# Setting up a graph kernel on one core: constants from few columns on three engines, and the first element's masks, positions and table made during its sort

## The chip, the cores and the metric

The kernel runs on one core of one Trainium2 chip. The metric is the device time of the whole program in microseconds (us). Engines are TensorE (PE, with PEld for its weight loads), VectorE (DVE), ScalarE (ACT), GpSimd (POOL) and SyncE (SP), which issues nearly all DMAs from one queue, in order.

## The reference, cut to what matters

Four layers run over 16 batch elements of 1024 nodes with 64 features and one adjacency matrix per element; each normalises x, applies relu, and adds its result to x. The change is in the first layer, which for every node aggregates weighted quantiles of its neighbours' features:

```python
adj_d = _dilate_adj(adj, mask)           # drops every skip-th neighbour of large rows
valid = adj_d > 0
sv = jnp.sort(jnp.where(valid[..., None], x[:, None, :, :], big), axis=2)
for tau, wt in zip([.25, .5, .75], [.25, .5, .25]):
    pos = jnp.clip(tau * (valid.sum(-1) - 1.0), 0.0)
    lo, hi = jnp.floor(pos), jnp.ceil(pos)
    agg += wt * (gather(lo) * (1 - (pos - lo)) + gather(hi) * (pos - lo))
y = relu((x + agg) @ W1 + b1) @ W2 + b2
```

Layer 1 is a mean over the adjacency, layer 2 an attention of eight heads biased by it, layer 3 a product with it.

## The kernel before, in words

**Order of work.** The program builds its constants, then two generators are woven by shares written by hand: `picks()` makes the first layer for all elements, `layers()` the other three. A scheduler orders the instructions of each engine by data and by buffers; each pool is a ring of buffers under one tag (`b2` has 6, `q4` 2, `a4` 4), so a new tile waits for what used its buffer.

**Constants (L127 to L352).** Selection matrices, identities, shifts and small columns. Nearly all are made by DVE: a pattern from POOL is widened to 128x128, its bits are reversed in integer steps (`bits_reversed`), compared and multiplied; `at_row` builds a column of per-row values by one comparison and one addition a row, then widens it. They use a scratch pool `scr`, which is closed before the main pool `sb` opens on the same memory. Weights are loaded by SP meanwhile; `rev`, the bit-reversed node numbers, is stored to DRAM as `rev_d`.

**First layer of an element.** The features of two elements share the 128 partitions. `ranked` normalises both, transposes them to `sv` and calls `ranks`. This is a bitonic sort of 1024 values per partition on DVE, 55 steps of compare, min and max (L577 to L579). Each step's comparison `sm` is stored to DRAM (`md`). The sorted values are stored as `vs_d`. Then the sort runs backward over the node numbers (`rev`, L609 to L612), reading the comparisons again (`sb`, two buffers of four steps each), which leaves each node's rank. TensorE transposes it; ACT copies it to `rs`, which is stored as `rk_d`. Beside the sort, in shares of two to one, `dilate` makes the thinned adjacency (`left_d`, `rem_d` in DRAM). For the first element both run alone.

Only then come the `stages` of the element: load its rank `rk`; for each half of the nodes, eight pairs of loads `lr` (L517, L521), TensorE's `pn`, and ACT's `valid` (fp8); counts `pm` by a product with ones, evicted as `m` (L640); positions `n`, `kq`, the rows `krow` (twelve ACT copies), `coef`; and from the sorted values `vs` the table `tab` by way of `put`, `u`, `pd` and `df`. `pair_weights` turns rank into weights `cw` (through `e`). `group` then counts with them (`px`, `high`, `low`, `cum`, `c`). The first comparison `le` (L819) with its products `wa` and `wb` opens the steady loop. For later elements stages and sort are spread behind the loop of the element before.

**The lines that the steps touch.** For the first element, before:

```python
els[0] = arrive(0)
for r in background(0):          # sort and dilate
    yield 0.0
for _ in els[0].stages:          # masks, positions, table
    pass
for pp in range(4):
    prepare(els[0], 0, pp)       # cw
for _ in make(els[0], 0, 0):     # first group
    yield 0.05
```

Of the kernel before, what the change touches and what calls it, by code (L numbers as in the profile page):

```python
# [8 lines left out]
F32 = mybir.dt.float32  # L9
# [29 lines left out]
def tile_preln_adj_stack(  # L39
# [87 lines left out]
    scr_i = sc("scr_i", (P, 5, P), I32)  # L127
    scr_f = sc("scr_f", (P, 3, P))
    identf = const.tile([P, P], F32, name="identf")
    make_identity(nc, identf)  # L130
    ident = const.tile([P, P], HP, name="ident")
    nc.vector.tensor_copy(ident, identf)

    rev_i = sc("rev_i", (P, C), I32)
    nc.gpsimd.iota(rev_i, pattern=[[1, C]], base=0, channel_multiplier=C)
    rev_a = sc("rev_a", (P, C), I32)
    rev_b = sc("rev_b", (P, C), I32)
    nc.vector.memset(rev_a, 0)
    for b_ in range(N.bit_length() - 1):
        up = N.bit_length() - 2 - 2 * b_  # L140
        nc.vector.tensor_scalar(
            rev_b, rev_i, 1 << b_, abs(up), op0=OP.bitwise_and,
            op1=OP.logical_shift_left if up >= 0 else OP.logical_shift_right,
        )
        nc.vector.tensor_tensor(rev_a, rev_a, rev_b, OP.bitwise_or)
    rev = sc("rev", (P, C), HP)
    nc.vector.tensor_copy(rev, rev_a)
    rev_d = dram.tile([P, C], HP, name="rev_d")
    nc.sync.dma_start(rev_d, rev)
    minus_i = const.tile([P, P], BF, name="minus_i")  # L150
    nc.vector.tensor_scalar(minus_i, identf, -1.0, None, op0=OP.mult)
# [3 lines left out]
    fmp_i = scr_i[:, 0, :]  # L155
    nc.gpsimd.iota(fmp_i, pattern=[[1, P]], base=0, channel_multiplier=-1)
    fmp = scr_f[:, 0, :]
    nc.vector.tensor_copy(fmp, fmp_i)


    step2 = sc("step2")
    nc.vector.scalar_tensor_tensor(step2, fmp, 2.0, identf, op0=OP.is_equal, op1=OP.subtract)
    dif = const.tile([P, 2, P], HP, name="dif")
    nc.vector.tensor_scalar(dif[:, 0, :], step2, -SPAN, None, op0=OP.mult)
    nc.vector.tensor_scalar(dif[:, 1, :], step2, -1.0, None, op0=OP.mult)
    less = const.tile([P, 2, P], HP, name="less")
    nc.vector.tensor_scalar(less[:, 0, :], identf, -2.0, None, op0=OP.mult)
    nc.vector.tensor_scalar(less[:, 1, :], identf, -FINE, None, op0=OP.mult)

    prow_i = scr_i[:, 1, :]  # L170
    nc.gpsimd.iota(prow_i, pattern=[[0, P]], base=0, channel_multiplier=1)
    fcol_i = scr_i[:, 2, :]
    nc.gpsimd.iota(fcol_i, pattern=[[1, P]], base=0, channel_multiplier=0)
    par_i = scr_i[:, 3, :]


    sel_w = const.tile([P, 2, 2 * BKW], HP, name="sel_w")
    nc.vector.tensor_scalar(par_i, prow_i, 1, None, op0=OP.bitwise_and)
    par = const.tile([P, 2], F32, name="par")
    nc.vector.tensor_copy(par[:, 1:2], par_i[:, 0:1])  # L180
    nc.vector.tensor_scalar(par[:, 0:1], par[:, 1:2], -1.0, 1.0, op0=OP.mult, op1=OP.add)
    par_up = const.tile([P, 2], F32, name="par_up")
    nc.vector.tensor_scalar(par_up, par, UP, None, op0=OP.mult)
    for c2 in range(2):
        cols = slice(c2 * BKW, (c2 + 1) * BKW)
        for i, w in enumerate((2.0, 2.0 * FINE)):
            nc.vector.tensor_scalar(
                sel_w[:, i, cols], fcol_i[:, :BKW], 0.0, w, op0=OP.mult, op1=OP.add
            )
            nc.vector.tensor_scalar(sel_w[:, i, cols], sel_w[:, i, cols], par[:, c2 : c2 + 1], None, op0=OP.mult)  # L190

    def bits_reversed(x, bits, n, name):
        r, u = sc(name + "_r", (P, n), I32), sc(name + "_u", (P, n), I32)
        nc.vector.memset(r, 0)
        for i in range(bits):
            up = bits - 1 - 2 * i
            nc.vector.tensor_scalar(
                u, x, 1 << i, abs(up), op0=OP.bitwise_and,
                op1=OP.logical_shift_left if up >= 0 else OP.logical_shift_right,
            )  # L200
            nc.vector.tensor_tensor(r, r, u, OP.bitwise_or)
        return r


    pblk = scr_i[:, 3, :]
    same = scr_f[:, 1, :]
    fblk = scr_i[:, 4, :]
    nc.vector.tensor_scalar(fblk, fcol_i, 4, None, op0=OP.logical_shift_right)
    fpl = sc("fpl", (P, P), I32)
    nc.vector.tensor_scalar(fpl, fcol_i, 15, None, op0=OP.bitwise_and)  # L210
    fplr = bits_reversed(fpl, 4, P, "fpl")
    ppl = sc("ppl", (P, P), I32)
    nc.vector.tensor_scalar(ppl, prow_i, 15, None, op0=OP.bitwise_and)
    pplr = bits_reversed(ppl, 4, P, "ppl")
    nc.vector.tensor_scalar(pblk, prow_i, 4, None, op0=OP.logical_shift_right)
    nc.vector.tensor_tensor(same, pblk, fblk, OP.is_equal)

    to30 = const.tile([P, 2], I32, name="to30")
    field = sc("field", (P, P))
    nc.vector.tensor_scalar(field, pplr, 15.0, None, op0=OP.is_equal)  # L220
    keep = sc("keep", (P, P))
    nc.vector.tensor_scalar(keep, field, -1.0, 1.0, op0=OP.mult, op1=OP.add)
    nc.vector.tensor_scalar(to30[:, 0:1], pplr[:, 0:1], 15.0, keep[:, 0:1], op0=OP.add, op1=OP.mult)
    nc.vector.tensor_scalar(
        to30[:, 1:2], field[:, 0:1], -65536.0 - 1073741824.0, 1073741824.0, op0=OP.mult, op1=OP.add
# [3 lines left out]
    tri = scr_f[:, 2, :]  # L229
    nc.vector.tensor_tensor(tri, pplr, fplr, OP.is_le)  # L230
    nc.vector.tensor_tensor(tri, tri, same, OP.mult)
    nc.vector.tensor_scalar(tri, tri, 0.5, None, op0=OP.mult)
    nc.vector.scalar_tensor_tensor(tri, identf, -40.5, tri, op0=OP.mult, op1=OP.add)
    nc.vector.tensor_tensor(tri, tri, keep, OP.mult)
    nc.vector.tensor_tensor(field, field, same, OP.mult)
    nc.vector.scalar_tensor_tensor(tri, field, 1.0 / KHI, tri, op0=OP.mult, op1=OP.add)
    nc.vector.tensor_scalar(field, fplr, 15.0, -0.5, op0=OP.is_equal, op1=OP.mult)
    nc.vector.tensor_scalar(field, field, 1.0, None, op0=OP.add)
    nth = const.tile([P, P], BF, name="nth")
    nc.vector.tensor_tensor(nth, tri, field, OP.mult)  # L240
# [3 lines left out]
    nc.vector.memset(sel_t, 0.0)  # L244
    for i in range(2):
        nc.vector.tensor_tensor(sel_t[:, i, 8 * i : 8 * i + 8], pblk[:, 0:8], fcol_i[:, 0:8], OP.is_equal)

    sel_c = const.tile([P, 8], F32, name="sel_c")
    nc.vector.tensor_scalar(pblk, prow_i, 7, None, op0=OP.bitwise_and)
    nc.vector.tensor_tensor(sel_c, pblk[:, 0:8], fcol_i[:, 0:8], OP.is_equal)  # L250
# [3 lines left out]
    fbk = sc("fbk", (P, P), I32)  # L254
    nc.vector.tensor_scalar(fbk, fcol_i, 1, None, op0=OP.logical_shift_right)
    pbk = sc("pbk", (P, P), I32)
    nc.vector.tensor_scalar(pbk, prow_i, 63, None, op0=OP.bitwise_and)
    pbkr = bits_reversed(pbk, 6, P, "pbk")
    for e in range(2):
        nc.vector.tensor_tensor(tab_d[:, e, :], fbk, pbkr, OP.is_equal)  # L260
    nc.vector.tensor_scalar(pbkr, pbkr, 1.0, None, op0=OP.add)
    fnx = sc("fnx", (P, P))
    nc.vector.tensor_tensor(fnx, fbk, pbkr, OP.is_equal)
    nc.vector.tensor_scalar(pbk, prow_i, 6, None, op0=OP.logical_shift_right)
    for e in range(2):
        nc.vector.tensor_tensor(tab_d[:, e, :], tab_d[:, e, :], fnx, OP.subtract)
        ph_ = sc("ph_", (P, P))
        nc.vector.tensor_scalar(ph_, pbk, float(e), None, op0=OP.is_equal)
        nc.vector.tensor_tensor(tab_d[:, e, :], tab_d[:, e, :], ph_, OP.mult)
# [4 lines left out]
    nc.vector.memset(none, 0.0)  # L274
    ones = const.tile([P, P], BF, name="ones")
    nc.vector.memset(ones, 1.0)

    k16 = const.tile([P, NBK, 2], HP, name="k16")
    nc.vector.tensor_scalar(
        k16.rearrange("p b s -> p (b s)"), fbk, 16.0, 15.0, op0=OP.mult, op1=OP.add  # L280
    )

    prow = sc("prow", (P, 1))
    nc.vector.tensor_copy(prow, prow_i[:, 0:1])
    off = sc("off", (P, 2))
    bkt = sc("bkt", (P, 1), I32)
    nc.vector.tensor_scalar(bkt, prow_i[:, 0:1], 1, None, op0=OP.logical_shift_right)
    nc.vector.tensor_scalar(off[:, 0:1], bkt, 8.0, -SHIFT, op0=OP.mult, op1=OP.add)
    nc.vector.tensor_scalar(off[:, 1:2], bkt, 0.0, None, op0=OP.is_equal)
    shifts = const.tile([P, 6], F32, name="shifts")  # L290
    nc.vector.tensor_scalar(
        shifts[:, 0:1], off[:, 0:1], -1.0, None, op0=OP.mult
    )
    nc.vector.tensor_scalar(
        shifts[:, 1:2], off[:, 0:1], -SPAN, None, op0=OP.mult
    )
    first = (FIRST - SHIFT) * SPAN / FINE
    rest_ = 8.0 * SPAN / FINE
    nc.vector.tensor_scalar(
        shifts[:, 2:3], off[:, 1:2], first - rest_, rest_, op0=OP.mult, op1=OP.add  # L300
    )
    nc.vector.tensor_scalar(shifts[:, 3:4], shifts[:, 2:3], FINE, None, op0=OP.mult)
    nc.vector.memset(shifts[:, 4:5], -0.5)
    nc.vector.memset(shifts[:, 5:6], 2.0 * (160.0 - FIRST) + 2.0)

    def at_row(dst, terms):

# [203 lines left out]
    def neighbours(left_d, rem_d, t):  # L511
# [3 lines left out]
        for j in range(C):  # L515
# [22 lines left out]
            if j < C - 1:  # L538
                yield None
        yield valid  # L540

    def ranks(V):

# [763 lines left out]
```

## Time and profile before

| what | us |
|---|---|
| median of 3 runs | 12679.28 (12668.32 to 12680.48) |
| profiled execution | 12671.61 |
| its span, first to last instruction | 12669.8 |
| DVE busy in the span | 11563.5 (91%), 19682 instructions |
| PE busy in the span | 11341.0 (90%), 84671 matmuls |
| ACT busy in the span | 9468.7 (75%) |
| first sort step on DVE | 42.75 |
| first backward step on DVE | 187.83 |
| rank's transposes on PE | 285.71 |
| first `le` on DVE | 346.18 |

The first four rows come from the runs and from the page's head and first part, the last four from the order of time over the first 370 us. Busy time is summed over the whole span; what one stage waits for is read from the stretch of that stage.

### The profile page before, as it was taken

Reading aid. Unit: us, or ns where it says so; the run is one execution under the profiler, and the core shown is the slowest. Engines: PE = TensorE matmul, PEld = TensorE weight load, DVE = VectorE, ACT = ScalarE, POOL = GpSimd, SP = SyncE. Lnnn points to the kernel's source line nnn. Section 1 sums busy time; section 2 is a strip of 40 time slices with the busy share of each in tenths; the row PEclk is TensorE's granted clock in tenths of the full one; section 3 lists DMA queues with packets and bytes.
Section 4 is the critical chain, followed back from the end, with each engine's and each line's share of the span. In section 5 each row is a group of like instructions: output and inputs, shape, how many; then the busy total and the mean of one; then the engine's idle time right before and its main releaser. Section 6 shows DMA issues by size and latency. Waiting matters only on the chain. (4 is left out here: it accounts for less than half of the span.)

```text
span 12669.8 us, 216982 instructions
## 1 busy us (share of the span) xinstructions
PE 11341.0 (90%) x84671; PEld 5347.0 (42%) x84673; DVE 11563.5 (91%) x19682; ACT 9468.7 (75%) x17028; POOL 1.3 (0%) x10
## 2 busy tenths in 40 slices
PE   0779999989899998999989999899998999999998
PEld 0224444444444444444444444444444444444445
DVE  8999989999898998999999999999999999988863
ACT  0557777778777777777877788777887877888866
POOL 0000000000000000000000000000000000000000
PEclk9999999999999999999999999999999999999999
DMA  3012121221212212121121212212121121302121
GB/s 105 28 41 70 52 87 53 66 78 59 83 54 72 73 55 83 53 91 57 57 83 53 94 56 67 76 61 85 56 90 52 64 84 56 99 30 66 34 72 60
DMA packets 503175, 841.07 MB, mean 66 GB/s; under 512 B 238720, under 2 KB 273664, under 8 KB 502144
## 3 DMA queue, kind: packets, MB, share of 16 engines
q1 hardware_dynamic: 502144, 827.20, 19.7%
q8 instruction: 662, 10.85, 0.3%
q14 instruction: 369, 3.02, 0.1%
HBM read 616.27 MB, written 206.57 MB: 65 GB/s over the span
## 5 line engine op out<-in xcount | busy, mean ns | idle before, releaser
L821 DVE TENSOR_TENSOR wa<-le,c 128x2048 f16<-128x2048 f16 x1536 | 1868.2, 1216 | 206.8 <-PE prep L842 173.6
L735 PE MATMUL px<-valid,cw 128*128 128x512 fp8e4 x8192 | 1979.9, 382 | 0.0
L819 DVE TENSOR_TENSOR le<-cum,krow 128x2048 f16<-128x2048 int16 x1536 | 1863.4, 1213 | 12.3 <-PE val L842 10.2
L823 DVE TENSOR_TENSOR wb<-le,c 128x2048 f16<-128x2048 f16 x1536 | 1866.8, 1215 | 1.2 <-PE prep L842 1.2
L406 ACT ACTIVATE c<-px,shifts 128x512 f16<-128x512 f32 x2048 | 1415.3, 698 | 278.9 <-PE px L756 139.0
L406 ACT ACTIVATE s<-s,nm 128x1024 f32<-128x1024 f32 x1024 | 1172.6, 1148 | 188.2 <-DVE nm L1199 184.6
L735 PEld LDWEIGHTS <-cw 128*128 128x128 f16 x8192 | 802.5, 98 | 1113.6 <-issue 231.2
L459 PE MATMUL pcols<-identf,s 128*128 128x128 f32 x8192 | 1168.9, 280 | 94.6 <-ACT eT L462 44.3
L1190 PE MATMUL sp<-kT,qT 64*128 64x512 f32 x4096 | 1166.2, 643 | 61.9 <-DVE nm L1199 59.4
L849 ACT COPY wi<-prep 128x512 f32<-128x512 f32 x1536 | 910.7, 593 | 373.1 <-PE prep L842 301.9
L842 PE MATMUL val<-le,tab 128*32 128x512 f16 x12288 | 1154.6, 386 | 18.1 <-DVE vs L869 7.3
L406 ACT ACTIVATE high<-px,shifts 128x512 f16<-128x512 f32 x1024 | 710.6, 694 | 602.5 <-PE px L735 599.3
L459 PEld LDWEIGHTS pcols<-identf,s 128*128 128x128 f32 x8192 | 900.2, 141 | 617.0 <-ACT eT L462 273.7
L869 DVE SCALAR_TENSOR_TENSOR vs<-pz,vs 128x512 f32<-128x512 f32 x1536 | 1046.6, 681 | 113.7 <-PE pz L862 110.7
L462 ACT COPY eT<-pcols 128x512 f32<-128x512 f32 x2048 | 1134.4, 604 | 20.8 <-PE pcols L459 18.1
L1213 PE MATMUL ao<-eT,v 128*64 128x128 f32 x16384 | 1080.2, 276 | 17.9 <-ACT eT L462 14.0
L406 ACT ACTIVATE vs<-val 128x512 f32<-128x512 f32 x1536 | 938.0, 611 | 161.5 <-PE val L842 108.2
L1213 PEld LDWEIGHTS ao<-eT,v 128*64 128x64 f32 x16384 | 907.5, 137 | 294.6 <-ACT eT L462 135.0
L1199 DVE CUSTOM_DVE_ANT_0 s<-sp,ad,nm 128x512 f32<-128x512 f32 x1024 | 725.9, 744 | 137.8 <-PE sp L1190 137.3
L857 DVE TENSOR_SCALAR bit<-wi,to 128x512 int32<-128x512 int32 x1536 | 826.3, 538 | 2.2 <-ACT cw L406 2.2
L842 PE MATMUL prep<-wb,sel_w 128*32 128x512 f16 x6144 | 650.4, 394 | 189.2 <-DVE wb L823 183.1
L1199 DVE CUSTOM_DVE_ANT_0 s<-sp,ad 128x512 f32<-128x512 f32 x1024 | 681.2, 682 | 128.8 <-PE sp L1190 104.8
(271 smaller groups left out, 18238.8 us busy)
## 6 DMA issues: line engine op xcount, KB each, us to landing
ad<-in_adj_dram SPq DMA_DIRECT2D x768, 512.0 KB
adjT_d<-aT SPq DMA_DIRECT2D x128, 512.0 KB
aT<-adjT_d SPq DMA_DIRECT2D x128, 512.0 KB
md<-sm SPq DMA_DIRECT2D x216, 256.0 KB
sb<-md SPq DMA_DIRECT2D x216, 256.0 KB
rem_d<-rem SPq DMA_DIRECT2D x128, 256.0 KB
left_d<-nb SPq DMA_DIRECT2D x128, 256.0 KB
lr<-left_d SPq DMA_DIRECT2D x256, 128.0 KB
```

What stands on the lines that cost most here:

```text
L406: nc.scalar.activation(out_, in_, func, **kw)
L459: nc.tensor.transpose(pt[:, c, :], ad[:, (4 * s + c) * P : (4 * s + c + 1) * P], identf)
L462: nc.scalar.copy(aT[:, 4 * s : 4 * s + 4, :], pt)
L735: yield nc.tensor.matmul(px[pp], w[:, j, :], valid[:, j, :], start=False, stop=j == C - 1, skip_group_check=True,)
L819: nc.vector.tensor_tensor(le, cum, bc(el.krow[q][:, None, hs], [P, 4, 512]), OP.is_lt)
L821: nc.vector.tensor_tensor(wa, le, c0, OP.mult)
L823: last = nc.vector.tensor_tensor(wb, le, c1, OP.mult)
L842: yield nc.tensor.matmul(dst[32 * pp : 32 * pp + 32, :], w[pp], r[pp], start=i == 2, stop=i in (1, 3), tile_position=(0, 32 * pp), skip_gr ...
L869: nc.vector.scalar_tensor_tensor(vs, pz, 80.0, vs, op0=OP.is_equal, op1=OP.mult)
L1190: nc.tensor.matmul(sps[e], qT[e * D : (e + 1) * D, i * P : (i + 1) * P], kT[e * D : (e + 1) * D, hs], start=True, stop=True,)
L1199: nc.vector.tensor_tensor_reduce(ss[e][:, hs], sps[e], ad[:, hs], -1.0, 3.0e38 if t == 0 else nms[e], op0=OP.add, op1=OP.min, accum_out=nm,)
L1213: nc.tensor.matmul(ao[e * D : (e + 1) * D, :], v[:, j, e * D : (e + 1) * D], eTs[e][:, j, :], start=j == 0, stop=j == C - 1, tile_position ...
```

## The change

**Constants.** They are made from few columns: seven bits of the partition number are taken apart once (`ci`, `cf`), and bit reversals are built from 128x1 columns (`rv`) and passed to 128x128 operations as per-partition scalars. Patterns along the free axis come from GpSimd in the order wanted. Memsets go to GpSimd. Scaled copies of the identity and the six widened `sel_q`, with `mid_w`, go to ScalarE. The store of `rev_d` is written behind the weights.

```diff
-    nc.vector.memset(rev_a, 0)
-    for b_ in range(N.bit_length() - 1):
...
-        nc.vector.tensor_tensor(rev_a, rev_a, rev_b, OP.bitwise_or)
+    rev_c = iota("rev_c", [(128, 2), (256, 2), (512, 2)])
...
+    for b_ in range(NB):
         nc.vector.tensor_scalar(
+            ci[:, b_ : b_ + 1], prow_i, b_, 1, op0=OP.logical_shift_right, op1=OP.bitwise_and
+        )
...
+    for b_ in range(1, NB):
+        nc.vector.scalar_tensor_tensor(
+            rv[:, b_ : b_ + 1], rv[:, b_ - 1 : b_], 2.0, cf[:, b_ : b_ + 1], op0=OP.mult, op1=OP.add
+        )
+    pplr, pbkr = rv[:, 3:4], rv[:, 5:6]
+    nc.vector.tensor_scalar(rev, rev_c, rv[:, 6:7], None, op0=OP.add)
...
+    def scaled(name, shape, dt, src, scale):
+        t = const.tile(list(shape), dt, name=name)
+        nc.scalar.activation(t, src, AF.Copy, scale=scale)
+        return t
...
     for q in range(NQ):
-        at_row(sel_q[:, q, :], ((q, -KHI), (R_TOP, ones_top * KHI), (R_MID, KHI)))
+        nc.scalar.activation(sel_q[:, q, :], qs[:, q + 1 : q + 2].to_broadcast([P, P]), AF.Copy)
...
-    nc.vector.memset(wproj, 0.0)
+    nc.gpsimd.memset(wproj, 0.0)
...
+    nc.sync.dma_start(rev_d, rev)
     scr.close()
```

**The first element.** When its `dilate` is done, its `stages` take that place in the two-to-one weave with the sort, so masks, positions and table are issued among the sort's last forward and its backward steps. Its sorted values and table use the `a4` buffers and not the `q4` of the comparisons. Its rank is copied by ScalarE straight from the transposes' PSUM tile (128x512) and not loaded from `rk_d`; the store of `rk_d` stays, for the second element. The stages of later elements are as before.

```diff
+        if own is not None:
+            own.rk = place("rk")
+            nc.scalar.copy(own.rk, pt[:, :, :D])
         rs = b2_("rs", (P, C, P), HP)
         nc.scalar.copy(rs, pt)
...
             except StopIteration:
                 going.remove(gen)
+                if b == 0 and gen is thinning:
+                    going.append(els[0].stages)
                 continue
...
-        el.rk = sb.tile([P, C, D], HP, tag="rk", bufs=2, name="rk")
-        nc.sync.dma_start(el.rk, rk_d[:, :, rows])
-        yield
+        pair = pairs[b // 2]
+        if b:
+            el.rk = place("rk")
+            nc.sync.dma_start(el.rk, pair[2][:, :, rows])
+            yield
...
-        vs = q4("vs")
-        nc.sync.dma_start(vs[rows, :], vs_d[rows, :])
-        table = sorted_table(s, vs)
+        while not pair:
+            yield
+        mine = q4 if b else a4
+        vs = mine("vs")
+        nc.sync.dma_start(vs[rows, :], pair[1][rows, :])
+        table = sorted_table(s, vs, mine)
```

## The prediction

> **What bounds the kernel now.** I read the page first, then the busy time by stretch over the first 370 us, then the waits of VectorE (DVE) there, then the order of time. All times below are from one profiled execution.
>
> ```profile
> PE 11341.0 (90%) x84671; PEld 5347.0 (42%) x84673; DVE 11563.5 (91%) x19682; ACT 9468.7 (75%) x17028; POOL 1.3 (0%) x10
> PE   0779999989899998999989999899998999999998
> ```
>
> TensorE and DVE are both nine tenths busy over nearly the whole span, except in the first slice (317 us), where TensorE does nothing. The change touches only what comes before the picks of the first batch element; behind them the instruction orders of the two built programs are the same on every engine. So what counts is the time of the first compare, `le` at 346.18 us: what the prologue gives, the end gets.
>
> ```profile
> 0.00:23.70 23.70, 0.00 (x0) 0.00 (x0) 22.84 (x221) 0.00 (x0) 1.35 (x10) 1.00 0.13 32
> 28.06:42.75 14.69, 1.97 (x8) 1.57 (x8) 8.29 (x29) 5.41 (x8) 0.00 (x0) 1.00 0.43 122
> 200.00:286.00 86.00, 0.28 (x3) 0.29 (x4) 80.92 (x199) 0.00 (x0) 0.00 (x0) 1.00 0.24 73
> 286.00:303.00 17.00, 10.66 (x57) 5.38 (x55) 0.00 (x0) 5.58 (x9) 0.00 (x0) 1.00 0.75 197
> 303.00:319.00 16.00, 10.29 (x65) 5.09 (x62) 8.29 (x15) 8.40 (x15) 0.00 (x0) 0.91 0.45 104
> 319.00:346.20 27.20, 19.70 (x59) 6.37 (x58) 9.28 (x25) 22.84 (x38) 0.00 (x0) 0.80 0.00 0
> ```
>
> The columns are the stretch, its length, busy time of PE, PEld, DVE, ACT and POOL, the granted clock, DMA share and GB/s. The reader is to see three stages in turn: constants on DVE alone (221 small instructions in 23.7 us); the sort, DVE alone, PE and ACT empty; and from 286 us the opposite, masks, positions, table and first group on PE and ACT with DVE idle for 17 us and two thirds of the rest. The waits say who DVE waits for in 40 to 346 us:
>
> ```profile
> DVE m L640 <- PE pm L637: 17.1, 1, 17.1
> DVE ve L427 <- ACT sq L406: 15.3, 2, 13.2
> DVE tab L695 <- ACT df L406: 7.5, 1, 7.5
> DVE sd L610 <- DMA sb<-md: 3.2, 1, 3.2
> ```
>
> **Part one, the constants.** The rows that set the start of the sort, in order of time:
>
> ```profile
> 9.03 0.35 SPq L149 DMA_DIRECT2D rev_d<-rev  x1
> 23.53 0.15 DVE L315 COPY q_tau<-row 128x1 f32<-128x1 f32 x1
> 23.75 0.33 SPq L394 DMA_DIRECT2D mk_u<-in_nodemask_dram  x1
> 24.14 0.43 SPq L947 DMA_DIRECT2D x<-in_x_dram  x1
> 28.06 0.67 DVE L420 TENSOR_REDUCE mean<-x 128x8 f32<-128x512 f32 x1
> 29.73 1.28 ACT L406 ACT_TABLE_LOAD   x1 [29.73 <-DVE w_one L352]
> ```
>
> SP is done with the weights at 9.0 but loads the mask and x only at 23.75: these tiles lie where the scratch pool lay, and DVE's last scratch operation is at 23.53. In the built order DVE has 244 constant instructions before the first `mean`, after the change 89; 13 copies stand on ACT, 14 patterns and memsets on POOL. 221 instructions took 22.9 us from DVE's start, 0.104 us each; 89 x 0.104 + 1.1 (it now starts with the first pattern) = 10.4 us. ACT: between `sd` (128x8, 0.21) and `sq` (128x512, 0.63) a 128x128 copy is some 0.3 us, 13 are 3.9 at most; the last six wait for `qs`, some three quarters through DVE's list, so ACT is done by 10. POOL: by its own rows (128x128 pattern 0.23, memset 0.20) under 3 us; `wproj`, now cleared there and loaded last on SP, is ready by 5. But `mk_u` also waits for the store of `rev` (a scratch tile) to land. `rev_d` stays behind all weights, at 9.0; a small DMA took at most 2.65 us here (`mk_u` at 23.75, its reader at 26.40), so `mk_u` can issue near 11.3 and SP, not DVE, is late next. The x load then follows as before: 23.75 - 11.3 = 12.4, and `mean` comes straight after the mask and not behind the end of the constants, 0.4 more.
>
> In the norm the first table load leaves the path, since ACT loads it for the constants. Row: the first `ve` stands 2.03 us after `d` is done (29.66 to 31.69), the second, without a load, 0.70 (36.47 to 37.17): 1.3 us. The Trainium skill, ScalarE: Activation LUTs, What ACT_TABLE_LOAD costs, adds a drain of some 1.38 us to the 1.28 of the load, 2.7 us in all; the trace has `sq` 0.02 us behind the load and no drain, so I take 1.3 (by the rule the gain would be 1.4 more). The interleaved leftovers at L349 and L352 go too, 0.4. The second x lies behind 1.5 MB of adjacency on SP as before; it lands some 8.7 us after its issue at the latest (26.18 to 34.86), and `mean` now asks for it 1.7 us earlier relative to that: 0.1 to 1 us, I take 0.2.
>
> One rule speaks against this part: the Trainium skill, SBUF — State Buffer, Who interferes with whom, says that copies, casts and tensor_scalar of DVE in a two-port mode and GpSimd's instructions lock each other out of a shared port for a whole instruction. The trace has POOL's patterns (1.30 to 1.90) beside DVE memsets only, at an unchanged 0.17 us, so it doesn't show the case. From both sides: nothing, or all of POOL's 3 us; up to 0.9 us of it is hidden by SP. I take nothing (by the rule in full, 2 us less).
> Sum of part one: 12.4 + 0.4 + 1.3 + 0.4 - 0.2 = **14.3 us earlier** (9 to 16).
>
> **Part two, what moves under the sort.** Forward pass: unchanged, 144 us of DVE. Behind it DVE waits for `rev` and the first `sb`. SP now passes two mask pairs (0.9 us each by their rows, 0.38 + 0.50) before them; only the second half of one stands between the last `md` (185.61) and `vs_d`, which waits for DVE until 186.8 anyway. I take +0.3 (0 to 1.5). In the backward pass each group of four steps (4 x 1.71 = 6.86 us) now has two of the 16 mask-load pairs behind each `sb` fetch on SP:
>
> ```profile
> SPq L597 <- DVE sd L610: 70.4, 12, 6.8
> ```
>
> SP sat waiting 70 of the 95 us for DVE to free an `sb` buffer; the loads add 14 x 0.9 = 13 us to a queue with that room. They stand behind the fetch of their own group, so the next fetch is late only if their own buffers are: those were freed three steps earlier. DMA share goes from 0.24 to about 0.5 (15 pairs made 0.75 of 17 us, 0.85 us a pair; two in 6.86 are 0.25). The load of `vs` moves up behind the second fetch; it needs `vs_d` landed, which the fetches ahead of it wait for already.
> On PE and ACT the moved work runs in 86 empty us: on ACT 16 `valid` of 0.6, `u`, four `df`, `kq` and 12 `krow`, some 20 us in all. I cost it at nothing; bare, it would be those 20.
> What DVE gains is work: `m` twice 0.69, `tab` 0.69 + 1.23 + 0.69, positions and `coef` 0.54 + 0.42 + 0.48 + 0.42 + 0.54 = 6.4 us; an independent neighbour starts 0.08 us before the end (L611 to L612 is 0.34 for 0.42), so +5.6. New wait: `m` stands in DVE's order, behind it the whole sort. Its eighth mask pair is issued behind the fetch four steps earlier: 1.7 us on SP, some 3 to 4 landing, 2 for `pn`, `valid`, `pm` (291.06 to 293.36) is about 7, against 6.86 + 0.4. It is about even, twice: +0.5 (0 to 5). Part two costs **6.4** (4 to 12).
>
> **Part three, behind the sort.** Before: 286.0 to 346.18, 60.2 us. After: transposes 0.75, the rank copied from PSUM by ACT 0.6 (128x512), then `e` and its clip for two pairs, 1.28 + 0.4; first `cw` starts 3.1 us behind the sort. Between first `cw` (318.15) and first `high` (324.49) lay 6.34 with two `krow` in it; now five `cw` back to back, 5 x 0.97 = 4.9. Then the row
>
> ```profile
> 325.07 5.88 ACT L406 ACTIVATE krow<-pkr,shifts 128x512 int16<-128x512 f32 x10
> ```
>
> leaves: `cum` comes 0.6 after `high` instead of 6.35. From `cum` (330.84) to `le` 15.3 stay; PE comes from idle and may run slow at first (eight `px` products took 3.53 us at 336.64, 1.89 at 342.38), which may hold the second `high` by 1 to 2 us, and has fewer pauses later: 0, with 2 either way. 3.1 + 4.9 + 0.6 + 15.3 = 23.9, say 24.3 with latencies: **35.9 earlier** (32 to 38). The store and reload of the rank (287.83 to 292) no longer precede `e`; the reload stays for the next element.
>
> **Sum.** -14.3 + 0.3 + 6.1 - 35.9 = **-43.8 us**; `le` near 302. This is against the profiled execution, 12671.6 us (span 12669.8 and 1.8 around it): 12627.8. The median of the runs shown is 7.7 higher, so 12635.
>
> **Rivals.**
> One, the masks come late. Each `m` stalls DVE and with it the sort, by 4 us, and fetches land a microsecond late seven times: 15 us. For it: the even sum above and `lr` packets mostly under 512 B. Against: SP's 70 idle us. 12650, chance 0.11.
> Two, the constants pay little: SP issues at its own pace and the `rev` store lands late, or POOL and DVE lock each other; `mk_u` at 17 and not 11: 12642, chance 0.06.
> Three, given back: 36 us at the end of the prologue shift the whole order, but a later stretch returns most of it (a lower clock of TensorE, or loads that come no earlier). Nothing in the identical orders says so; 12670, chance 0.05.
> Four, slower: SP turns serial. If each `sb` fetch has to wait until the mask pair ahead of it has landed and been read, the fetch (4.2 us, 187.19 to 191.43) and the pair (2.4, 288.67 to 291.06) lie bare in each of 13 groups: 13 x 6.6 = 86, with 6 of DVE work against 50 gained, +42: 12721. It decides from 5.3 us a group on (13 x 5.3 = 50 - 6 + 25). Against: fetches have a second buffer. Chance 0.02.
>
> **How the numbers follow.** The forecast has 0.76, with 12622 to 12648 of its own. 0.2% is 25 us, about what can be told from no change. Faster by more: forecast, one and two, 0.93; within: three, 0.05; slower: four, 0.02. The range 12620 to 12652 adds both bounds of part one and two and some 5 us of run to run (12668 to 12680), and takes in rivals one and two.
>
> **What would show it.** Right: `mk_u` near 11 us on SP; first sort step near 28; `m`, `tab`, `coef` among the backward sort steps with no idle over 1 us before them; sort end near 278; `le` near 302; `krow` wholly before the sort's end; the stretch behind `le` as long as before within 10 us. Wrong: idle before `sb` readers or `m` adding to over 10 us, or a span that shrinks by far less than `le` moves.

## The result, and the profile after

| what | before | after |
|---|---|---|
| median of 8 runs each | 12680.17 (12666.16 to 12688.10) | 12639.99 (12630.58 to 12653.04) |
| ratio, 95% interval | | 0.9970 (0.9959 to 0.9981) |
| profiled execution | 12671.61 | 12653.04 |
| its span | 12669.8 | 12651.3 |

The medians lie 40.2 us apart. The profiled execution of after is the slowest of its eight, so its span understates the gain; what it lost, and where, is settled below by a second one. Times are in us throughout.

From the page, the busy times and TensorE's row of slices:

```profile
PE 11366.1 (90%) x84671; PEld 5353.3 (42%) x84673; DVE 11552.0 (91%) x19522; ACT 9473.1 (75%) x17042; POOL 3.2 (0%) x20
PE   2789989999899998999989999899998999999998
```

DVE lost 160 instructions and only 11.5 us of work: the gain is not in doing less. It is in the first slice, which was empty on PE and now has work. The busy time by stretch shows the same stages as before the change: constants, norm, backward pass, the pause behind the sort, the tail to the first `le`. The columns are the stretch, its length, busy time of PE, PEld, DVE, ACT and POOL, the granted clock, DMA share and GB/s.

```profile
0.00:9.80 9.80, 0.00 (x0) 0.00 (x0) 8.65 (x88) 4.09 (x14) 3.20 (x20) 1.00 0.25 64
15.29:29.55 14.26, 1.97 (x8) 1.56 (x8) 7.93 (x23) 4.13 (x7) 0.00 (x0) 1.00 0.56 145
179.37:280.80 101.43, 32.76 (x114) 13.00 (x115) 93.96 (x229) 19.19 (x32) 0.00 (x0) 0.71 0.38 109
280.80:283.87 3.07, 0.75 (x8) 0.49 (x5) 1.66 (x4) 1.50 (x2) 0.00 (x0) 0.50 0.00 0
283.87:306.55 22.68, 16.49 (x46) 5.68 (x47) 10.25 (x25) 16.74 (x26) 0.00 (x0) 0.72 0.12 29
```

The constants take 9.8 and not 23.7. The backward pass, where PE and ACT were empty, carries 32.8 of PE and 19.2 of ACT, at 7 us more length. The two stretches behind the sort make 25.8 where 60.2 were. The third column from the right is what the prediction had put at 0, with 2 either way: PE's granted clock is 0.50 and 0.72 there.

The waits of DVE from 26 to 310 us (line and tile, what it waited for, us in total, times, longest):

```profile
DVE ve L400 <- ACT sq L379: 9.7, 2, 7.8
DVE sd L585 <- DMA rev<-rev_d: 3.4, 1, 3.4
...
DVE sd L586 <- DMA sb<-md: 1.9, 1, 1.9
DVE tab L674 <- ACT df L379: 1.7, 1, 1.7
...
DVE m L619 <- PE pm L616: 0.3, 1, 0.3
```

The 17.1 for `m` have become 0.3 and the 7.5 for `tab` 1.7. `rev` is up from 1.0 to 3.4, and `sb` down from 3.2 to 1.9. The wait of 7.8 for `sq` is the next pair's norm behind the first group's copies; the first `le` doesn't wait for it.

All runs, cut at the same events in their traces: the first sort step; the turn (from the end of the last forward step to the first product with `sb`); the backward pass (from there to the end of its last `sr`); the tail (from there to the first `le`). The forward pass took 144.0 to 144.1 in all of them.

| kernel | first sort step | turn | backward | tail | first le |
|---|---|---|---|---|---|
| before | 42.75 | 4.6 | 94.6 | 60.2 | 346.18 |
| after | 29.55 | 5.7 | 101.4 | 25.8 | 306.55 |
| after, a second profile | 30.01 | 6.3 | 101.5 | 25.0 | 306.82 |
| constants alone | 29.88 | 4.7 | 94.6 | 60.3 | 333.45 |
| stages alone | 42.79 | 6.5 | 101.5 | 24.9 | 319.74 |
| mask loads doubled | 29.95 | 5.6 | 101.6 | 24.6 | 305.85 |
| rank from DRAM | 29.95 | 5.5 | 100.5 | 29.0 | 309.00 |
| table in q4 | 29.80 | 5.6 | 100.5 | 24.9 | 304.86 |
| early x | 21.81 | 6.1 | 100.8 | 24.3 | 297.06 |
| PE kept busy under the sort | 30.04 | 6.0 | 100.6 | 27.3 | 307.93 |
| and in the pause behind it | 29.48 | 6.5 | 101.1 | 23.9 | 305.12 |
| early x, PE kept busy in both | 22.20 | 6.0 | 101.6 | 24.0 | 297.89 |
| early x, rank from DRAM | 21.63 | 5.9 | 102.2 | 30.5 | 304.31 |

Six of these kernels (mask loads doubled, rank from DRAM, table in q4, early x, and PE kept busy in one place and in two) were timed once each; of them only the traces are used.

### The profile page after: what moved, and what is told of

The parts are those of the page before. It is cut to its first block, busy times and chain, and to the rows that moved or that the text cites. A ratio compares the mean times of both kernels' runs of the same rounds, so it can differ in the third digit from the quotient of the medians.

```text
span 12651.3 us, 216854 instructions
## 1 busy us (share of the span) xinstructions
PE 11366.1 (90%) x84671; PEld 5353.3 (42%) x84673; DVE 11552.0 (91%) x19522; ACT 9473.1 (75%) x17042; POOL 3.2 (0%) x20
```

## The experiments

### One part at a time

**Constants alone**: the kernel before with the new constants.

> The kernel before with the constants of the change alone (part one); stages and rank as before. Theory (two independent gains): the first mean comes 12 to 13 us earlier, near 15.3, the first sort step 13.2 earlier, near 29.5, and the first le carries exactly that, near 333 us instead of 346.2, the tail behind the sort staying 60 us long; median about -13 us, which is under what one run can tell but not under the mean of five rounds. Rival two of the prediction (the constants pay little): first mean later than 20 us and le later than 340. A third possibility, that the earlier start is lost at the turn because rev is loaded later: the sort's end less than 11 us earlier.

First mean 16.15, first sort step 12.9 earlier, turn, backward pass and tail as before to 0.1, first `le` 12.7 earlier. The median was 12660.64 against 12670.20, ratio 0.9995 (0.9987 to 1.0003), an interval that takes in both no change and the 13 us expected: this part alone is below what runs can tell, but the trace places it. Rival two (the constants pay little) is out, and so is a loss at the turn.

**Stages alone**: the kernel before with the masks, positions and table under the sort, and the rank copied from PSUM.

```diff
             except StopIteration:
                 going.remove(gen)
+                if b == 0 and gen is thinning:
+                    going.append(els[0].stages)
                 continue
```

> The kernel before with the first element's masks, positions and table under its sort (parts two and three); constants as before. Theory: start of the sort as before (first sort step 42.7), sort's backward pass 7 us longer (94.6 to about 101.5), the tail to le 34 us shorter (60.2 to about 26), turn between the passes 1 us longer: le near 320 us, -26; median about -26. The sum of this run and of the run with the constants alone should be the whole change, -40. Rival: the two parts help each other or collide (the mask loads meet a later rev load): le differs from 346.2 - 26.4 by more than 3 us.

First `le` at 319.74, 26.4 earlier; median 12645.57 against 12670.20, ratio 0.9981 (0.9973 to 0.9988). The two parts add: 12.7 + 26.4 = 39.1 against 39.4 and 39.6 for the whole change. To half a microsecond they don't help or hinder each other.

### Is the lead kept?

In the first profile of after the lead shrank evenly from 39.6 at the first `le` to 13.4 at the last, though the orders of instructions behind it are the same. This looks like rival three.

> The kernel after once more, unchanged, for a second profiled execution and a time on the chip of these runs. In the first profile the lead at the first le, 39.6 us, had shrunk to 13.4 at the last le; the medians lost nothing. Theory (the loss belongs to that one execution, the slowest of its eight): here the lead at the first le is again within 0.5 us of 39.6 and the lead at the last le within 10 us of it, the median some 40 us below the kernel before. Rival three of the prediction (given back by the change itself): the lead shrinks again by 20 us or more in the same even way.

The second profile led by 39.4 at the first `le`, by 34.3 at the last and by 39.1 at the end of the span (the first profile: 39.6, 13.4 and 18.5). The median was 12634.74 against 12674.14, 39.4 apart, ratio 0.9968 (0.9956 to 0.9980). So the change gives nothing back that can be told; what the first profile lost is its own. The busy time between the same two `le` (the 193rd and the 1153rd) says of what kind it is; the lines are of before, of the first profile of after and of the second:

```profile
1729.20:9339.20 7610.00, 7002.66 (x52748) 3302.77 (x52748) 7177.72 (x12134) 5898.26 (x10617) 0.00 (x0) 0.99 0.21 69
```
```profile
1690.80:9321.50 7630.70, 7020.05 (x52745) 3309.68 (x52744) 7182.62 (x12134) 5898.35 (x10617) 0.00 (x0) 0.98 0.21 69
```
```profile
1689.60:9302.30 7612.70, 7005.41 (x52746) 3307.08 (x52744) 7181.44 (x12134) 5897.32 (x10617) 0.00 (x0) 0.99 0.21 69
```

The same work; in the first profile of after PE is busy for 15 to 17 us longer with as many products, at a granted clock of 0.98 and not 0.99, while DVE has 1 to 5 us more and ACT at most 1. The loss belongs to that execution and points to TensorE's clock in it; what lowered the clock there is not shown.

One trap lies here: the mean clock of the whole span is lower in both profiles of after (0.977 and 0.978) than before (0.981). The first 346 us have most of this, before and after:

```profile
0.00:346.00 346.00, 43.35 (x186) 18.88 (x187) 284.94 (x799) 51.22 (x76) 1.35 (x10) 0.98 0.31 96
```
```profile
0.00:346.00 346.00, 87.79 (x367) 33.13 (x368) 303.59 (x693) 82.29 (x135) 3.20 (x20) 0.89 0.32 100
```

0.09 x 346 / 12650 = 0.0025. But TensorE is not slower for it. In before the column stands at 1.00 from the start to 316 us, with PE idle for most of that time, and the products contradict it; both of these lines of before lie in stretches that it gives as 1.00:

```profile
298.22 0.63 PE L531 MATMUL pn<-ident,lr 128*128 128x128 f16 x4
300.02 0.39 PE L531 MATMUL pn<-ident,lr 128*128 128x128 f16 x4
```

The same four products took 0.63 up to there and 0.39 behind. After the change it is alike: 0.63 under a column of 1.00 up to 211 us, 0.39 at 217. So in these profiles the column says nothing of the speed until its first fall, at 316 us in before and at 218 in after, and that shift accounts for the lower mean. How fast TensorE ran before that is read from the length of like products. Where its half clock under the sort does cost something is shown at `tab`, below.

### Is SP's queue near its limit?

**Mask loads doubled.** Each of the first element's 16 mask pairs is loaded a second time.

```diff
             nc.sync.dma_start(lr[:, 1, :], rem_d[j, :, hs])
+            if not once:
+                spare = sb.tile([P, 2, 512], BF, tag="att", bufs=1, name="spare")
+                nc.sync.dma_start(
+                    spare[:, 0, :].rearrange("i (c j) -> i c j", c=4),
+                    left_d[4 * t : 4 * t + 4, :, j * P : (j + 1) * P].rearrange("c i j -> i c j"),
+                )
+                nc.sync.dma_start(spare[:, 1, :], rem_d[j, :, hs])
```

> The kernel after, with each of the first element's 16 mask pairs loaded a second time into a spare tile that nobody reads: the loads that the change put on SP's queue under the sort are doubled. Theory (SP has room: it waited 70 of 95 us for VectorE before): the 16 extra pairs of some 0.9 us add 14 us to SP and cost VectorE next to nothing, the sort's end stays within 2 us of 280.8. Rivals one and four (masks or fetches come late): each m waits 2 us or more and the fetches sb up to 2 us in each of 13 groups, the sort's end 6 to 26 us later.

The sort ended at 281.24 against 280.80 and 281.84 in the two profiles of after, its backward pass took 101.6 against 101.4 and 101.5. SP's own waits for a freed `sb` buffer, of after and of this kernel:

```profile
SPq L573 <- DVE sd L586: 60.7, 12, 8.0
```
```profile
SPq L582 <- DVE sd L595: 53.7, 12, 8.1
```

The change took 10 of the 70 us that SP had to spare, the doubling 7 more. Rivals one and four need this wait to be near nothing; it is not.

### Details of the change, undone

**Table in q4.** The sorted values, `u` and `df` go to the two buffers of the comparisons.

```diff
-        mine = q4 if b else a4
+        mine = q4
```

> The kernel after, with the first element's sorted values, u and df in the two buffers of the comparisons (q4), as the kernel before had them, and not in a4. It undoes one detail of the change. Theory (the fetches of comparisons need both buffers, so the table can only be made when the last fetch has been read): vs is loaded behind the last fetch, tab comes in the last steps of the sort and VectorE waits there for df by 3 to 8 us; the sort's end 3 to 8 us later, krow partly behind it, le 5 to 12 us later. Rival: it costs nothing, le within 1 us, since the table is not needed before val.

The theory failed, and the rival was right that it costs nothing: the first `le` came 1.7 to 2.0 earlier. The table did come later, its first `tab` at 243.5 and not at 214.95, but far from the end, and DVE didn't wait for it there. In the kernel after it does; DVE's order of time:

```profile
212.88 0.42 DVE L588 TENSOR_TENSOR sr<-sr,sd 128x512 f16<-128x512 f16 x1
214.95 0.69 DVE L674 CAST tab<-df 128x1024 f16<-128x1024 f32 x1 [1.65 <-ACT df L379]
215.56 0.42 DVE L585 TENSOR_TENSOR sd<-sr 128x512 f16<-128x512 f16 x1
```

`tab` stands in front of a sort step that is ready, and holds it for 1.65. In the run with `q4` no row of `tab` waits. But 1.65 is not the price of the `a4` buffers: with them, the run with the rank from DRAM waits 0.69 at the same place, and its backward pass is as short as with `q4` (100.5). Behind `df` stand TensorE's products `pd`; the second pair, in after and in that run:

```profile
211.93 2.08 PE L663 MATMUL pd<-u,tab_d 128*128 128x512 f32 x2
```
```profile
212.20 1.12 PE L663 MATMUL pd<-u,tab_d 128*128 128x512 f32 x2
```

The same products took 0.96 less, and `tab` waited 0.96 less. The four `pn` products next to them take 0.63 or 0.39 in the same way. In all ten profiles that have the table in `a4` a pair of 2.04 to 2.08 goes with a wait of 1.60 to 1.65, one of 1.12 to 1.18 with 0.69 to 0.75, and pairs between with waits between. So TensorE's half clock makes up 0.96 of the wait, and whether a kernel meets it differs from profile to profile; 0.9 to 1.0 of what `q4` seems to gain lies within that. What is left of the gain is in the turn, the tail and the sort's start and isn't told apart. The part of the change that gives the table buffers of its own buys nothing here.

**Rank from DRAM.** `rk` is stored and loaded again, as before the change.

```diff
-        if own is not None:
-            own.rk = place("rk")
-            nc.scalar.copy(own.rk, pt[:, :, :D])
...
         nc.sync.dma_start(rk, rs)
+        if own is not None:
+            own.rk = place("rk")
+            nc.sync.dma_start(own.rk, rk[:, :, :D])
```

> The kernel after, but the first element's rank goes back to what it did before: stored as rk_d and loaded from there, not copied by ScalarE out of the transposes' PSUM tile. Theory: the shortcut is worth one store and one load, 4 to 5 us (287.8 to 292 us in the kernel before), all on the path: the first cw comes near 288 instead of 283.9 and le near 311 instead of 306.6. Rival: TensorE, slow at first (granted 0.50 and 0.72 of full speed behind the sort), is what sets the tail, and the extra wait changes le by under 2 us or, if the clock falls further in the longer pause, by more than 6.

DVE's first `e` in after and here:

```profile
282.21 1.29 DVE L684 TENSOR_TENSOR e<-k,rk 128x1024 f16<-128x1024 f16 x2 [1.41 <-ACT rk L599]
```
```profile
286.70 1.29 DVE L684 TENSOR_TENSOR e<-k,rk 128x1024 f16<-128x1024 f16 x2 [2.91 <-DMA rk<-rk_d]
```

From the sort's end the first `e` comes 6.7 later instead of 1.4, so the copy is worth 5.3 there. The first `le` moved by 2.45 only. The sort ended 0.8 earlier (the `pd` and `tab` above), and PE, later at work, was granted the full clock from 294 on, where in after it fell back from 293 and the second set of `px` ran at half clock: the first `high` waited 0.37 for `px` and not 2.12, and the second set took 1.89 and not 3.33. At the sixteenth and the seventeenth `le` this kernel was even 2.7 ahead of after: while DVE waited for the rank it did the next pair's norm. The theory's size held for the rank, not for `le`.

### What is late next: x

**Early x.** Both x of the first pair are SP's first loads, into the memory of the attention's weights, which are loaded later; the node mask is made behind the norm.

```diff
+    wqkv = const.tile([P, 2 * H * D], F32, name="wqkv")
+    early = [wqkv[:, s * 512 : (s + 1) * 512].rearrange("p (c d) -> p c d", d=D) for s in range(2)]
+    for s in range(2):
+        nc.sync.dma_start(early[s], x[s].rearrange("(c p) d -> p c d", p=P))
...
```

> The kernel after, with x of the first pair loaded first of all on SP, into the memory that the weights of the attention take later, and the node mask made behind the norm. Theory (SP's late start, not VectorE's constants, sets the norm: 15.3 us for the first mean with the constants done at 9.7): the first mean comes near 10, the first sort step near 24 instead of 29.6, the sort's end and the first le each 5 to 6 us earlier, le near 301. Rival: the norm waits for its share of VectorE or ScalarE (sel_q copies), the first mean comes but the sort starts under 3 us earlier; or the later weights push the first md stores and the sort waits for them.

The first sort step came at 21.81, 7.7 earlier, the first `le` 9.5 earlier: more than expected. Of the 9.5, 7.7 are in the start of the sort: with both x there the two norms are interleaved and fill each other's waits. The other 1.8 are mostly `tab` (it waited 0.75) and the tail (24.3), and both differ by about as much among the profiles of the kernels that share them. The first mean came at 11.63 and not near 10, since it still waited, now for the store of `rev`:

```profile
11.63 1.28 DVE L397 TENSOR_REDUCE mean<-wqkv 128x8 f32<-128x512 f32 x2 [1.77 <-DMA rev_d<-rev]
```

The mean's output lies where the scratch pool lay, and that memory is free only when the store has landed. So the order of what is late is: store of `rev` (11.5), mask and x behind it (15.3), second x (21.7), while DVE's constants are done at 9.8, before all of them.

### What is late in the tail: TensorE's clock

**PE kept busy under the sort.** Four products of 128x512 more in each of the last four backward steps.

```diff
+            if own is not None and n < 4:
+                pw = pb("warm")
+                for _ in range(4):
+                    nc.tensor.matmul(pw, ident, R[:, :512], start=True, stop=True)
```

> The kernel after, with four products of 128x512 more, into a PSUM tile that nobody reads, in each of the last four backward steps of the first sort, so that TensorE is busy before the tail begins. It takes out the one term of the tail that the prediction left at 0 plus or minus 2. Theory (TensorE granted 0.50 and 0.72 behind the sort holds the tail back: px took 6.0 us for 16 and 3.3 for 8, where 8 take 1.9 at full clock): the clock behind the sort is near 1.00, high comes 2 us and le 2 to 4 us earlier, near 303. Rival: ScalarE's row of cw sets the tail (4.84 us for five), and le moves by under 1 us.

The first `le` came 1.4 later than in after: the expectation failed. The busy time by stretches of 2 us says why (the third column from the right is the clock):

```profile
280.00:282.00 2.00, 2.00 (x11) 0.78 (x10) 0.68 (x2) 0.00 (x0) 0.00 (x0) 0.70 0.00 0
282.00:284.00 2.00, 0.42 (x8) 0.24 (x5) 0.93 (x2) 1.50 (x2) 0.00 (x0) 1.00 0.00 0
284.00:286.00 2.00, 0.15 (x1) 0.13 (x2) 2.00 (x5) 1.26 (x2) 0.00 (x0) 0.65 0.35 131
286.00:288.00 2.00, 2.00 (x6) 0.65 (x5) 2.00 (x5) 2.00 (x3) 0.00 (x0) 0.50 0.30 48
```

The products did raise the clock, at about 281, 5.6 us after the first of them; and 3.4 us without work (from the transposes to `px`) threw it back to 0.50 just when `px` began.

**And in the pause behind it.** Ten more products on the rank's copy fill that pause.

> The kernel after with the 16 products under the last four steps of the sort (as in the run with them alone, where the granted clock rose to 1.00 at 282 us and was 0.50 again from 285) and ten more on the rank's copy, so that the pause between the transposes and px is filled too. All of these products go to a PSUM tile that nobody reads. Theory (TensorE is granted 0.50 after a pause of some 3 us[...]): now px starts at 1.00, the wait of the first high for px falls from 2.1 us to under 0.7 (the copies cw then set the pace), le comes 1 to 3 us earlier than in the kernel after, 303.5 to 305.5. Rival: px is slow for another reason (weights loaded between its products) and stays at 6 us for 16; le as before or later by what the ten products take.

TensorE's order of time, first of after, then of this kernel:

```profile
280.52 1.04 PE L595 MATMUL pr<-ident,sr 128*128 128x128 f16 x8 [32.54 <-DVE sr L587]
284.99 6.03 PE L714 MATMUL px<-valid,cw 128*128 128x512 fp8e4 x16 [3.43 <-ACT cw L379]
...
297.22 3.33 PE L714 MATMUL px<-valid,cw 128*128 128x512 fp8e4 x8
...
302.75 1.89 PE L714 MATMUL px<-valid,cw 128*128 128x512 fp8e4 x8
```
```profile
282.10 0.61 PE L599 MATMUL pr<-ident,sr 128*128 128x128 f16 x8
283.38 2.32 PE L606 MATMUL warm<-rk,ident 128*128 128x512 f16 x10 [0.67 <-ACT rk L603]
286.14 3.63 PE L723 MATMUL px<-valid,cw 128*128 128x512 fp8e4 x16 [0.44 <-ACT cw L379]
```

`px` took 3.6 and not 6.0, and ACT's first `high` no longer waits; of after, then of this kernel:

```profile
290.84 0.69 ACT L379 ACTIVATE high<-px,shifts 128x512 f16<-128x512 f32 x1 [2.12 <-PE px L714]
```
```profile
289.78 0.67 ACT L379 ACTIVATE high<-px,shifts 128x512 f16<-128x512 f32 x1
```

In the eight other runs with these stages that show the sixteen in one row they took 5.3 to 6.4, so 3.6 is no scatter. From the first `cw` to `le` it is 20.1 where after has 22.7 and 21.9. The net is less: the products stand in PE's queue in front of the transposes and delay them (they start 0.9 behind the sort's end, and not with it). The first `le` comes at 305.12, inside the expected range and 1.4 to 1.7 earlier, which alone would not tell, as two kernels without such products have it at 304.9 and 305.9; the tail of 23.9 is the shortest of all, against 24.3 to 25.8 in those that copy the rank and have no such products. Within this case PE was granted 0.50 after idling and 1.00 from 2.9 to 5.6 us after its work began, and lost it within a pause of 3.4; in after it also lost it at 293, between short products. That fits what the Trainium skill, TensorE: Matmul & The Clock Gate, Part 1, states of it (half clock by default, full after a busy window of about 3.4 us that runs on its own, half again after an idle one). The scatter may be that of the window's phase against the work, which no run here separates.

### A version that combines them

**Early x, and PE kept busy in both places.**

> The kernel after with x of the first pair loaded first (as in the run that had this alone: first le 297.1 instead of 306.6) and both sets of extra products that keep TensorE busy. Theory: the gains add up where they are on the path: le at 295 to 297, the median some 10 us below the kernel after, about 50 below the kernel before. Rival: the extra products delay the transposes or px, or the earlier x had already put px at full clock: le no earlier than 297, median 8 us below the kernel after; or the gain behind le is lost in the loop, median within 5 us of the kernel after.

First `le` at 297.89; median 12626.75 against 12673.22, 46.5 below the kernel before, ratio 0.9964 (0.9950 to 0.9977). It beats the kernel before; beside after, whose ratio in the comparison above was 0.9968 (0.9956 to 0.9980), the intervals overlap, and only the trace (8.7 to 8.9 at the first `le`) tells them apart. The extra products earned nothing here: the first `le` is 0.8 later than with the early x alone. The sort starts 0.4 later, the turn is 0.2 shorter, and the backward pass is 0.8 longer, with more waits at `m` and `tab`. The transposes wait for the products by 1.0, and the tail is only 0.3 shorter. On this point the rival was right.

**Early x, and the rank from DRAM.**

> The kernel after with x of the first pair loaded first, and the first element's rank loaded from DRAM and not copied from PSUM. In the run with the rank from DRAM alone the first le was 2.5 us later than in the kernel after, but the sixteenth 2.7 us earlier, since VectorE had done the next pair's norm and first sort steps while it waited. Theory (what counts is VectorE's work done, not the first le): le near 299.5, later than with the early x alone, but the sixteenth le 2 to 3 us earlier than there, the median some 11 us below the kernel after, 50 below the kernel before. Rival (the first le is what counts, and the order of the first group was luck): the sixteenth le too is later than with the early x alone, the median 7 us below the kernel after.

Median 12631.07, ratio 0.9966 (0.9953 to 0.9978). The first `le` at 304.31 was 7.2 later than with the early x alone, and the sixteenth and seventeenth still 2.1 later, where the theory had it 2 to 3 earlier. The rival's sign came true, but the order was not luck: from the first `le` to the sixteenth it won 5.1 here (7.2 late became 2.1 late), and 5.1 in the earlier run (2.45 late became 2.7 ahead). What differs is what the rank's way through DRAM cost before the first `le`. Beside its partner each time, the sort ended 0.8 earlier in the earlier run and 1.1 later in this one, and the tail grew by 3.2 there and by 6.2 here, where PE fell back to 0.50 from 293 to 295 and in the earlier run did not.

## Why the prediction was right, point by point

The forecast's mechanism and its size held: 43.8 predicted to the first `le`, 39.6 measured; median 12635 predicted, 12640 and 12634.7 measured. The terms of the sum:

| step of the prediction | predicted | measured | what it was |
|---|---|---|---|
| part one, first sort step | -14.3 | -13.2 | second x; the leftovers saved nothing |
| turn | +0.3 | +1.1 | `sb` landed later; why is not shown |
| backward pass | +6.1 | +6.9 | wait before `tab`, not `m`; `pd` at half clock |
| part three, tail | -35.9 | -34.4 | `px` at half clock |
| first le | -43.8 | -39.6 | |

All four terms came out worse than forecast, by 0.8 to 1.5 each, so nothing cancelled in the sum.

**Part one.** In order of time:

```profile
9.49 0.55 SPq L361 DMA_DIRECT2D rev_d<-rev  x1
9.68 0.16 DVE L324 TENSOR_TENSOR w_frac<-rq_f 128x1 f32<-128x1 f32 x1
11.49 0.34 SPq L367 DMA_DIRECT2D mk_u<-in_nodemask_dram  x1
15.29 0.68 DVE L393 TENSOR_REDUCE mean<-x 128x8 f32<-128x512 f32 x1
21.66 0.69 DVE L393 TENSOR_REDUCE mean<-x 128x8 f32<-128x512 f32 x1 [0.67 <-DMA x<-in_x_dram]
```

`mk_u` was put at 11.3 because the store of `rev` has to land; it was 11.49, with DVE's last constant at 9.68. That it came so near is in part luck: the store was issued at 9.49 and not 9.0, and `mk_u` went 2.0 behind it, where the prediction's own 2.65 for a small DMA would have made 11.7 from 9.0. The first mean gained 12.77, the predicted 12.4 + 0.4. From the first mean to the second it was 6.80 and became 6.37, 0.4 gained where 1.3 + 0.4 - 0.2 = 1.5 were forecast: the table load did leave (the first `ve` stands 0.84 behind `d`, not 2.03, so 1.2, as the trace had said, and not the 2.7 of the rule that the prediction cites), but DVE then ran into the second x, 0.67 and not 0.2, and the leftovers at L349 and L352 had cost nothing: from the first `mean` to `d` it is 0.91 before and after. Behind the second mean nothing changed (7.89 to the first sort step in both). A gain in front of a load that is late anyway is paid out only in part. GpSimd did hold DVE up once, which the prediction took as nothing: on DVE `sel_w` took 0.54 after 0.17 for its twin, beside the clearing of `wproj` by POOL (3.23 to 3.75), and both it and `cfac` behind it end just after that. It cost nothing, since SP was late, not DVE. Two patterns of POOL took 0.45 and 0.44 where two others of 128x128 took 0.24 and 0.26; but those two alone repeat every value twice in a row, so this may be their form and not DVE.

**Turn.** The first `sb` fetch was issued 0.69 behind the last forward step, before the change 0.41: that is the +0.3. The rest is landing: 5.05 from issue to reader where it was 4.24. A mask load, `rev` and `vs_d` go out just ahead of it; which of them delays it is not shown, and with the mask loads doubled the turn was no longer (5.6). Also `rev` itself is late now. SP's queue, of before and of after:

```profile
184.10 0.37 SPq L588 DMA_DIRECT2D rev<-rev_d  x1
185.61 0.32 SPq L581 DMA_DIRECT2D md<-sm  x1
```
```profile
172.46 0.32 SPq L557 DMA_DIRECT2D md<-sm  x1
172.82 0.43 SPq L494 DMA_DIRECT2D lr<-rem_d  x1
173.30 0.45 SPq L564 DMA_DIRECT2D rev<-rev_d  x1
173.85 0.38 SPq L561 DMA_DIRECT2D vs_d<-sv  x1
```

It stood ahead of the last `md` and was issued 2.7 before the forward pass ended; now it stands behind that store, which has to wait for the last comparison, and behind a mask load, and goes 0.3 before the end. DVE waits 3.4 for it. This costs little only because `sb` is later still. With the stages under the sort the turn took 5.5 to 6.5 in all runs, without them 4.6 and 4.7.

**Backward pass.** Predicted: 5.6 of work and 0.5 of stalls, both at `m`. Measured: stalls 0.29 at the first `m`, none at the second, and 1.65 at `tab`, of which the prediction had said nothing; that leaves 4.9 of work. "No idle over 1 us before them" failed for `tab`. The step that the prediction had wrong here is the work moved to PE and ACT, "I cost it at nothing": DVE's `tab` waits for it, and 0.96 of the wait is `pd` at half clock, as shown above.

**Tail.** The first `cw` came 3.07 behind the sort (3.1 predicted), five `cw` took 4.84 (4.9), `cum` followed 0.58 behind `high` (0.6), and from `cum` to `le` it was 15.1 (15.3). The one term that failed is the one put at "0, with 2 either way": `px` at half clock, 2.12. Filled with work, the wait went. It is the same cause as at `tab`. (One reading of the profile before was loose: DVE idles three fifths of the time from 303 to 346, not two thirds; no term rests on it.)

**The rivals.** One (masks late): `m` waited 0.3, and doubling the loads left the sort's end where it was. Two: `mk_u` at 11.49 and not 17. Three: the medians keep 40.2 and 39.4 of 39.6 and 39.4. Four: SP still waits 60.7 us for DVE. One sign failed in one profile: the stretch behind `le` was to stay as long within 10 us, and to the end of the span it was 21.1 longer in the first profile of after; in the second it was 0.3 longer.

## What to carry to other kernels

Here a prologue in front of a loop whose order doesn't change was worth its whole length: measure to the first instruction of the loop, cut by cut, and single microseconds can be read that runs, 22 us apart here, never show. Where the order behind it does change, the first instruction misleads: with the rank from DRAM 5.1 of the loss was won back by the sixteenth `le`. Move work under a stage whose engine is the only one busy, and then look at three places for what comes back: the in-order instruction that now waits in front of ready work (`tab`), the load that moved back in the DMA queue (`rev`), and the engine that starts its stage from idle at half clock. Filling an idle TensorE helped here only when the filler reached up to the first useful product, and it stood in the queue ahead of whatever came with it.

## What was not expected of the hardware

TensorE's clock behind the sort: sixteen products took 6.0 us after a pause and 3.6 without one, and products that ended 3.4 us too early were useless. Under the sort the same clock made `pd` take 2.08 or 1.12, and DVE waited for the difference. The profile's clock column read 1.00 up to 218 us (before the change 316), though like products still took 0.63 and not 0.39 at 211 (at 298). And one execution of the same program ran its loop 0.2% slower (7630.7 against 7612.7 between the same two instructions), with more time in TensorE as the only large difference, which in a single profile looks just like a gain that is given back.
